# Cross-attention on one core: weights head by head ahead of the context, and larger pieces for Wv and x

## The chip, the cores and the metric

The kernel runs on one core of a Trainium2 chip. The metric is device time in microseconds (us), the median of several executions. Durations come from one profiled execution on the chip. PE is the matmul engine (PEld its weight loads, which overlap with its matmuls), DVE, ACT and POOL are the vector, scalar and general engines, SP is the engine that issues the DMA transfers; a name with q (SPq) is the engine's own sequencer.

## What is computed

One layer of cross-attention, all in float32, with B = 16, 256 queries of width 256 a batch, 77 keys of width 192 a batch, H = 8 heads of D = 256:

```python
Q = (img_embed @ Wq).reshape(B, -1, H, D).transpose(0, 2, 1, 3)
K = (sent_embed @ Wk).reshape(B, -1, H, D).transpose(0, 2, 1, 3)
V = (sent_embed @ Wv).reshape(B, -1, H, D).transpose(0, 2, 1, 3)
score = jnp.einsum('bhqd,bhkd->bhqk', Q, K) / math.sqrt(D)
score = jnp.where(mask, score, -jnp.inf)
attn = jax.nn.softmax(score, axis=-1)
ctx = jnp.einsum('bhqk,bhkd->bqhd', attn, V).reshape(B, -1, H * D)
out = ctx @ Wo + img_embed
return (out - mu) * jax.lax.rsqrt(var + EPS) * gamma + beta
```

img_embed is x (16 x 256 x 256), sent_embed the context (16 x 77 x 192), and the mask has one integer per key.

## The kernel before

The kernel multiplies weights together first. For each head, G = Wk Wq^T / 16 (192 x 256) takes the place of Wq and Wk, and U = Wv Wo (192 x 256) that of Wv and Wo. The 192 rows are held as 128 (A: gA, uA) and 64 (B: gB, uB). Then for a batch, a = G^T c^T (keys turned into the width of x), scores = x a, and the output is attention times vw = c U, plus x, normalised.

**Start (L441 to L621).** The transfers are issued in this order, all on SP but the first: the first two of eleven context blocks on ACT (L449), the other nine (L450), Wq and Wk for head 0, then head 1, then two heads at a time (L453 to L459), Wv in 24 transfers of pieces of 128 bytes (L460 to L468, already laid out for DVE's transposes of 32x32 blocks), Wo in four (L469), the mask (L472), and x of the first group of four batches, turned by blocks, in eight transfers of 128-byte pieces (L475, L155). PE's order is written by hand: 20 transposes of the identity that keep it busy (L484), the context's transposes pc (L492), then by head the transposes of Wq and Wk (p_wqT and p_wkT, L524) and the product pg (L538), one head of transposes ahead; then the B rows of G for all heads (ph, L548), a of the first group (pa, L186 and L200), U's A rows (pu, L538) and B rows (pw, L548), and the last 13 keys' vw of all batches (pr, L265 and L273), which go by way of a scratch in DRAM into vr (L287, L292). Between these, ACT and DVE in turn copy results out of PSUM (L138, L140); DVE turns Wv in place (wvT, L584) between the two halves of pa's copies and x (xT, L164) before pr's. POOL copies the second halves of cB and uB (L503, L599) and then computes the additive mask, bias (L602 to L617).

**Main loop (L632).** For each batch: scores of two tiles of 128 queries (ps, L306, 128x32 tiles of PE), shift and maximum (L320, L327, L328), exponential (L335), vw of the next batch (pv, L228 and L239), a quarter of the next group's a (pa), weights (L341 to L349), turned on DVE (L359), attention times vw (po, L371), and normalisation (L383 to L428). x of the next group is loaded once a group (load_xT) and turned on DVE.

All PSUM tiles come from one ring of eight banks, so a matmul that begins a tile waits until the tile of eight allocations earlier has been copied out. A float32 matmul is two records in the profile. A form like 64*32 after the names is the tile of PE's array that the instruction uses: rows by columns; instructions on different tiles run at once. Tiles that carry the same tag share storage: wo's load waits until the weights that lay there have been read, and the tiles for x's rows (xg) are first used for the turned Wq and Wk.

The U stage of before, L535 to L540 with L586 to L594, computes one head at a time over 128 rows:

```python
of_weights(pu[:, h % 2, :], wvT[:, h], slice(P), lambda dc: wo_part(h, dc))
```

Of the kernel before, what the change touches and what calls it, by code (L numbers as in the profile page):

```python
# [8 lines left out]
F32 = mybir.dt.float32  # L9
I32 = mybir.dt.int32  # L10
AF = mybir.ActivationFunctionType
ALU = mybir.AluOpType
# [33 lines left out]
def kernel(  # L46
# [25 lines left out]
    KR = S2 - KM  # L72
    BK = 32
    NM = P // BK
    PW = (NF + 1) * BK
    RB = 8
    assert KM == 2 * BK and NM == NF and 2 * KR <= BK
# [48 lines left out]
    def half(i):  # L126
        return slice(i * LB, (i + 1) * LB)
# [18 lines left out]
    def in_two(name, shape, g):  # L146
        return pools[g % 2].tile(shape, F32, tag=f"{name}{g % 2}", name=f"{name}_{g}", bufs=1)

    def load_blocks(dst, src):

        dst = dst.rearrange("p a (m q) -> p a m q", q=BK)
        src = src.rearrange("(m r) (a i q) -> a i r m q", r=BK, q=BK, i=P // BK)
        for a in range(dst.shape[1]):
            for i in range(P // BK):
                nc.sync.dma_start(dst[i * BK : (i + 1) * BK, a], src[a, i])  # L155

    def load_xT(g):
        xT_of[g] = in_two("xT", [P, 2, GT * P], g)
        load_blocks(xT_of[g], x.rearrange("b s d -> (b s) d")[g * GT * P : (g + 1) * GT * P, :])

    def transpose_x(g, j):

        cols = xT_of[g][:, :, j * P : (j + 2) * P]
        nc.vector.transpose(cols, cols)  # L164


# [2 lines left out]
    def prepare_a(g, pairs, B_first=False):  # L169
# [6 lines left out]
        banks = []  # L176

        def cols(dc, i):
            return slice(dc * P + i * BK, dc * P + (i + 1) * BK)

        def part_A():
            if not B_first:
# [115 lines left out]
    def scores(t):  # L298
        g = t // GT
        j, bl = t % GT, (t // QT) % GB  # L300
        ps = [ps_mm.tile([P, 512], F32, tag="mm", name=f"ps_{t}_{a}") for a in range(2)]
        for m in range(NM):
            q = j * P + m * BK
            for dc in range(2):
                for i in range(NM):
                    nc.tensor.matmul(  # L306
                        ps[m // 2][i * BK : (i + 1) * BK, m % 2 * 2 * S2 : (m % 2 + 1) * 2 * S2],
                        xT_of[g][:, dc, q : q + BK],
                        flat(a_of[g][:, dc, bl, 2 * i : 2 * i + 2, :]),
                        start=(dc == 0),  # L310
                        stop=(dc == 1),
                    )
        ps_of[t] = ps
# [126 lines left out]

    early = ctx.enter_context(tc.tile_pool(name="early", bufs=1))  # L441
    pools[0] = turned = early
    with tc.tile_pool(name="wload", bufs=4) as ring, tc.tile_pool(name="wonce", bufs=1) as wp:
        c_sb = wp.tile([CR, NCR, DL], F32, tag="c", name="c_sb")
        wq_r = wq.rearrange("(t p) f -> p t f", p=P)
        wk_r = wk.rearrange("(t p) f -> p t f", p=LP)
        wo_r = wo.rearrange("(t p) f -> p t f", p=P)
        first = 2
        nc.scalar.dma_start(c_sb[:, :first, :], c_rows[:, :first, :])  # L449
        nc.sync.dma_start(c_sb[:, first:, :], c_rows[:, first:, :])  # L450
        wq_of, wk_of, wo_of = {}, {}, {}
        wvT = wp.tile([P, H, 2, DL], F32, tag="wvT", name="wvT")
        for n in range(NF):  # L453
            wq_of[n] = ring.tile([P, 2, 2 * D], F32, tag="w128", name=f"wq_{n}")
            wk_of[n] = ring.tile([LP, 2, 2 * D], F32, tag="w96", name=f"wk_{n}")
            for lo, hi in ((0, D), (D, 2 * D)) if n == 0 else ((0, 2 * D),):
                cols = slice(2 * n * D + lo, 2 * n * D + hi)
                nc.sync.dma_start(wq_of[n][:, :, lo:hi], wq_r[:, :, cols])
                nc.sync.dma_start(wk_of[n][:, :, lo:hi], wk_r[:, :, cols])  # L459
        wv_blocks = wv.rearrange("(m r) (a i q) -> m i r a q", r=BK, q=BK, i=NM)  # L460
        for m in range(DL // BK):
            for i in range(NM):
                nc.sync.dma_start(
                    wvT.rearrange("p h a l -> p (h a) l")[
                        i * BK : (i + 1) * BK, :, m * BK : (m + 1) * BK
                    ],
                    wv_blocks[m, i],
                )  # L468
        for n in range(NF):  # L469
            wo_of[n] = ring.tile([P, 4, DI], F32, tag="w128", name=f"wo_{n}")  # L470
            nc.sync.dma_start(wo_of[n], wo_r[:, 4 * n : 4 * n + 4, :])
        nc.sync.dma_start(  # L472
            bias_f.bitcast(I32), mask.rearrange("b k -> (b k)").partition_broadcast(P)
        )
# [6 lines left out]
            for i in range(n):  # L481
                nc.tensor.transpose(idle, ident, ident)

        keep_busy(20)  # L484
        for r in range(0, NCR, 2):
            if r == first:
                keep_busy(2)
            n = min(2, NCR - r)
            pc = ps_mm.tile([P, 4, P], F32, tag="mm", name=f"pc_{r}")
            for lc in range(2):  # L490
# [15 lines left out]

        nc.gpsimd.memset(vr, 0.0)


        wqT_of = [  # L510
            const.tile([P, H // 2, 2, DI], F32, tag=f"xg{i}", name=f"wqT_{i}") for i in range(2)
        ]
        wkT_of = [
            const.tile([P, H // 2, 2, DL], F32, tag=f"xg{i + 2}", name=f"wkT_{i}") for i in range(2)
        ]
        wqT = [wqT_of[h * 2 // H][:, h % (H // 2)] for h in range(H)]
        wkT = [wkT_of[h * 2 // H][:, h % (H // 2)] for h in range(H)]

        def turn_weight(dst, w_of, rows, h, tag):
            pt = ps_mm.tile([P, 4, P], F32, tag="mm", name=f"p_{tag}_{h}")  # L520
            for dc in range(2):
                for r in range(2):
                    lo = h % 2 * D + dc * P
                    nc.tensor.transpose(  # L524
                        pt[:, 2 * dc + r, :rows],
                        w_of[h // 2][:, r, lo : lo + P],
                        ident[:rows, :rows],
                    )
            evacuate(dst.rearrange("p a (r n) -> p (a r) n", r=2), pt[:, :, :rows])

        def turn_qk(h):
            turn_weight(wqT[h], wq_of, P, h, "wqT")
            turn_weight(wkT[h], wk_of, LP, h, "wkT")

        def of_weights(out, tT, rows, moving):  # L535

            for dc in range(2):
                nc.tensor.matmul(  # L538
                    out, tT[:, dc, rows], moving(dc), start=(dc == 0), stop=(dc == 1)
                )  # L540

        def rest_of_weights(tT, moving, name):

            banks = [ps_mm.tile([P, DI], F32, tag="mm", name=f"{name}_{n}") for n in range(NF)]
            for n in range(NF):
                for dc in range(2):
                    for i in range(2):
                        nc.tensor.matmul(  # L548
                            banks[n][half(i)],
                            tT[2 * n + i][:, dc, P:],  # L550
                            moving(2 * n + i, dc),
                            start=(dc == 0),
                            stop=(dc == 1),
                        )
            return banks

        turn_qk(0)
        for h in range(H):
            if h + 1 < H:
                turn_qk(h + 1)  # L560
            if h % 2 == 0:
                pg = ps_mm.tile([P, 2, DI], F32, tag="mm", name=f"pg_{h}")
            of_weights(pg[:, h % 2, :], wkT[h], slice(P), lambda dc: wqT[h][:, dc, :])
            if h % 2:
                nc.scalar.mul(gA[:, h - 1 : h + 1, :], pg, D ** -0.5)
        for n, pg in enumerate(rest_of_weights(wkT, lambda h, dc: wqT[h][:, dc, :], "ph")):
            if n % 2:
                nc.scalar.mul(gB[:, n, :], pg, D ** -0.5)
            else:
                nc.vector.tensor_scalar(gB[:, n, :], pg, D ** -0.5, None, ALU.mult)  # L570
        for g in range(NG):
            load_x(g)
            if g == 0:
# [3 lines left out]
        for n in range(0, NF, 2):  # L577
            part_A, part_B, copies = prepare_a(0, (n, n + 1), B_first=(n > 0))
            for part in (part_A, part_B)[:: -1 if n else 1]:
                part()  # L580
            for dst, src in copies():
                evacuate(dst, src)
            for h in range(2 * n, 2 * n + 4, 2):
                nc.vector.transpose(wvT[:, h : h + 2], wvT[:, h : h + 2])  # L584

        def wo_part(h, dc):  # L586
            return wo_of[h // 2][:, h % 2 * 2 + dc, :]

        for h in range(H):
            if h % 2 == 0:  # L590
                pu = ps_mm.tile([P, 2, DI], F32, tag="mm", name=f"pu_{h}")
            of_weights(pu[:, h % 2, :], wvT[:, h], slice(P), lambda dc: wo_part(h, dc))
            if h % 2:
                evacuate(uA[:, h - 1 : h + 1, :], pu)  # L594
        for n, pu in enumerate(rest_of_weights([wvT[:, h] for h in range(H)], wo_part, "pw")):
            for i, engine in enumerate((nc.scalar.copy, nc.vector.tensor_copy)):
                h = 2 * n + i
                engine(uB[half(i), h, :], pu[half(i)])  # L598
                nc.gpsimd.tensor_copy(uB[half(1 - i), h, :], uB[half(i), h, :])  # L599


        nc.gpsimd.tensor_scalar(bias_f, bias_f.bitcast(I32), 0.0, None, ALU.is_equal)  # L602
# [123 lines left out]
```

## Time and profile before

| | |
|---|---|
| median of 3 runs | 290.67 us (290.58 to 290.76) |
| profiled execution | 290.27 us |
| its span, first to last instruction | 288.4 us |
| PE busy | 278.7 us (97%) |
| DVE, POOL, ACT busy | 206.3, 123.7, 118.2 us |
| mean granted PE clock | 0.992 |
| DMA, mean over the span | 90 GB/s, 64377 packets, 46905 of them under 512 bytes |
| start, up to the first scores (ps) | 0 to 61.35 us |
| main loop, last PE row | to 272.18 us |
| end on DVE and ACT | to 288.4 us |

The span lies 1.9 us below the profiled execution's time, and that time 0.4 us below the median of the runs. A row of the chain of waits is start, length and what; a row of the timeline is start, length, engine, line, operation, output<-input, tile and shapes, count, and in brackets the idle time before it and what ended it; a row of the windows is stretch and length, then the busy time of PE, PEld, DVE, ACT and POOL with counts, the granted clock, the DMA engines' busy share and GB/s.

### The profile page before, as it was taken

The numbers are of one execution on the slowest core, as the hardware profiler recorded it, in microseconds if no ns is written. First come the engines' busy times: TensorE is split into PE (matmuls) and PEld (weight loads), VectorE is DVE, ScalarE is ACT, GpSimd is POOL, SyncE is SP. The second block draws the span as 40 slices with busy tenths as digits, with TensorE's granted clock in tenths as the row PEclk, the third lists the DMA queues.
The fourth block names the chain that finished last, engine by engine and source line by source line (L and its number), as shares of the span: only waits on it lengthen the run. The fifth ranks groups of instructions, "written<-read, shape, count | busy, mean of one in ns | idle before, by whom it ended". The sixth has DMA issues, their size and how long they took to land.

```text
span 288.4 us, 11416 instructions
## 1 busy us (share of the span) xinstructions
PE 278.7 (97%) x5132; PEld 177.5 (62%) x5132; DVE 206.3 (72%) x412; ACT 118.2 (41%) x203; POOL 123.7 (43%) x156
## 2 busy tenths in 40 slices
PE   8899999999999999999999999999999999999990
PEld 8795567364656575757575757575757567576550
DVE  0531453435768798989797989897979898898884
ACT  2452232032353535353535353535353534735531
POOL 1800002986554334344334242534342527658562
PEclk9999999999999999999999999999999999999996
DMA  7986798895859401910101009200000000010112
GB/s 201 314 193 95 143 328 117 244 352 147 189 141 139 81 4 39 139 47 5 37 5 35 6 28 142 47 13 25 18 22 22 19 22 24 19 40 2 39 39 73
DMA packets 64377, 25.90 MB, mean 90 GB/s; under 512 B 46905, under 2 KB 62857, under 8 KB 64329
## 3 DMA queue, kind: packets, MB, share of 16 engines
q1 hardware_dynamic: 64088, 25.01, 36.8%
q8 instruction: 40, 0.66, 1.0%
q10 hardware_dynamic: 240, 0.17, 0.2%
q14 instruction: 9, 0.07, 0.1%
HBM read 19.27 MB, written 5.90 MB: 87 GB/s over the span
## 4 chain that ended last, share of the span: by engine, by line
PE 90%; DVE 3%; DMA 3%; SPq 1%; ACT 1%; issue 1%; POOL 0%; POOLq 0%
PE ps L306 23%; PE po L371 22%; PE pa L186 12%; PE pv L228 10%; PE pa L200 6%; PE pv L239 6%; DMA wk<-in_L_xattn_Wk_dram 3%; PE pu L538 2%; PE pr L265 2%; PE pg L538 2%; PE pr L273 1%; PE ph L548 1%; PE pw L548 1%; PE p_wqT L524 1%; PE p_wkT L524 1%; DVE bn L385 1%
## 5 line engine op out<-in xcount | busy, mean ns | idle before, releaser
L328 POOL TENSOR_TENSOR s<-s,top 128x616 f32<-128x616 f32 x32 | 39.0, 1218 | 85.0 <-DVE top L327 77.2
L306 PE MATMUL ps<-a,xT 128*32 128x154 f32 x2048 | 70.0, 294 | 0.0
L306 PEld LDWEIGHTS ps<-a,xT 128*32 128x32 f32 x2048 | 66.4, 110 | 4.0 <-ACT stage L138 0.8
L349 POOL TENSOR_TENSOR p<-e,rden 128x512 f32<-128x512 f32 x64 | 50.4, 808 | 28.6 <-ACT a L664 25.5
L371 PE MATMUL po<-vw,pT 128*32 128x256 f32 x1024 | 61.5, 380 | 0.0
L371 PEld LDWEIGHTS po<-vw,pT 128*32 128x32 f32 x1024 | 31.8, 110 | 28.2 <-issue 5.5
L341 DVE TENSOR_REDUCE den<-e 128x8 f32<-128x616 f32 x32 | 25.5, 795 | 24.2 <-ACT e L335 24.2
L335 ACT ACTIVATE e<-s 128x616 f32<-128x616 f32 x32 | 23.0, 719 | 32.1 <-POOL s L328 32.1
L186 PE MATMUL pa<-cA,gA 128*32 128x308 f32 x512 | 35.8, 423 | 0.0
L320 DVE TENSOR_TENSOR s<-ps,bias 128x308 f32<-128x308 f32 x64 | 27.6, 464 | 7.3 <-POOL bias L617 4.7
L662 ACT COPY vw<-pv 128x512 f32<-128x512 f32 x32 | 18.6, 581 | 32.2 <-PE pv L239 32.2
L228 PE MATMUL pv<-uA,cA 128*32 128x512 f32 x256 | 30.4, 592 | 0.0
L186 PEld LDWEIGHTS pa<-cA,gA 128*32 128x32 f32 x512 | 16.4, 110 | 21.0 <-issue 6.6
L428 DVE SCALAR_TENSOR_TENSOR xg<-xg,rstd,bet 128x256 f32<-128x256 f32 x26 | 28.0, 1078 | 0.9
L396 ACT ACTIVATE std<-mv,eps 128x2 f32<-128x2 f32 (+1 forms) x17 | 5.0, 296 | 57.2 <-DVE mv L388 57.2
L359 DVE STREAM_TRANSPOSE pT<-p 128x640 f32<-128x640 f32 x32 | 25.1, 812 | 2.4 <-POOL p L349 2.4
L327 DVE TENSOR_REDUCE top<-s 128x8 f32<-128x616 f32 x32 | 25.4, 795 | 1.1
L371 PE MATMUL po<-vr,pT 128*32 128x256 f32 x256 | 19.7, 379 | 0.0
L396 ACT ACT_TABLE_LOAD x15 | 19.2, 1283 | 0.3
L200 PE MATMUL pa<-cB,gB 64*32 64x308 f32 x512 | 19.3, 419 | 0.0
L335 ACT ACT_TABLE_LOAD x14 | 18.0, 1283 | 0.2
L599 POOL COPY uB<-uB 64x256 f32<-64x256 f32 x8 | 3.2, 397 | 34.7 <-ACT uB L598 34.3
(75 smaller groups left out, 288.2 us busy)
## 6 DMA issues: line engine op xcount, KB each, us to landing
xT<-in_x_dram SPq DMA_DIRECT2D x32, 128.0 KB
xg<-in_x_dram SPq DMA_DIRECT2D x4, 1024.0 KB
out_dram<-xg SPq DMA_DIRECT2D x15, 256.0 KB
wo<-in_L_xattn_Wo_dram SPq DMA_DIRECT2D x4, 512.0 KB
scratch<-stage SPq DMA_DIRECT2D x16, 104.0 KB
vr<-scratch SPq DMA_DIRECT2D x8, 208.0 KB
wq<-in_L_xattn_Wq_dram SPq DMA_DIRECT2D x3, 512.0 KB
wvT<-in_L_xattn_Wv_dram SPq DMA_DIRECT2D x24, 64.0 KB
```

Of the source, the lines that this page charges most:

```text
L186: nc.tensor.matmul(flat(o[i * BK : (i + 1) * BK]), gA[:, h, cols(dc, i)], flat(cA[:, batches, :]), start=not B_first, stop=B_first,)
L200: nc.tensor.matmul(flat(banks[j + k][i * BK : (i + 1) * BK]), gB[half(k), h // 2, cols(dc, i)], flat(cB[half(k), batches, :]), start=B_fir ...
L228: nc.tensor.matmul(pv[k][i * BK : (i + 1) * BK], cA[:, b, k * BK : (k + 1) * BK], flat(uA[:, heads[i], :]), start=True, stop=False,)
L306: nc.tensor.matmul(ps[m // 2][i * BK : (i + 1) * BK, m % 2 * 2 * S2 : (m % 2 + 1) * 2 * S2], xT_of[g][:, dc, q : q + BK], flat(a_of[g][:, ...
L320: nc.vector.tensor_tensor(s[:, a * H // 2 : (a + 1) * H // 2], ps[a][:, : H // 2 * S2].rearrange("p (h k) -> p h k", k=S2), bias[:, b, :]. ...
L327: nc.vector.tensor_reduce(top, s, AX.X, ALU.max)
L328: nc.gpsimd.tensor_tensor(s, s, top.unsqueeze(2).to_broadcast([P, H, S2]), ALU.subtract)
L335: nc.scalar.activation(e, s_of.pop(t), AF.Exp)
L341: nc.vector.tensor_reduce(den, e, AX.X, ALU.add)
L349: nc.gpsimd.tensor_tensor(part, e_mh[:, :, :, keys], rden_mh.unsqueeze(3).to_broadcast(list(part.shape)), ALU.mult,)
L371: nc.tensor.matmul(po[i * BK : (i + 1) * BK], pT[:, n, i], vw_of[b][:, n // 2, n % 2, :] if n < NF else vr[:, b, :], start=(n == 0), stop= ...
L428: nc.vector.scalar_tensor_tensor(y, y, rstd, bet, ALU.mult, ALU.add)
```

## The change

- SP issues Wq and Wk of each head as two transfers (pieces of 1 KB), heads 0 to 7, and only then the whole context in one transfer. They go into wq_all and wk_all, one tile each.
- Wv comes in 16 transfers with pieces of 512 bytes: each piece is 128 consecutive columns of a row of Wv. DVE turns it in place in blocks of 32x32 whose elements lie 16 bytes apart. Wo comes with four consecutive rows (4 KB) to a partition, into wo_all, which shares storage with wq_all.
- 14 identity transposes instead of 20, and none between the context blocks. PE begins with the weights; ph is done after heads 3 and 7 for two pairs each; the context's transposes follow G.
- U is computed for two heads at once: rows 0 to 63 of the array are one head and rows 64 to 127 the other, four steps n over the contraction, and the output in blocks of 32 columns (64*32 tiles). The two heads write to different banks. pw likewise, two pairs of heads at a time.
- x of a group comes in four transfers with pieces of 256 bytes instead of eight with pieces of 128. The order of its columns in blocks changes, and gA's columns (cols in prepare_a) with it.
- One Exp of one column is put at the start on ACT.

The core of the diff:

```diff
     def load_xT(g):
-        xT_of[g] = in_two("xT", [P, 2, GT * P], g)
-        load_blocks(xT_of[g], x.rearrange("b s d -> (b s) d")[g * GT * P : (g + 1) * GT * P, :])
+        xT_of[g] = in_two("xT", [P, GT * NM, 2, BK], g)
+        rows = x.rearrange("b s d -> (b s) d")[g * GT * P : (g + 1) * GT * P, :]
+        rows = rows.rearrange("(m r) (i n) -> i r m n", r=BK, i=NM)
+        for i in range(NM):
+            nc.sync.dma_start(
+                xT_of[g][i * BK : (i + 1) * BK].rearrange("p m n q -> p m (n q)"), rows[i]
+            )
...
-            return slice(dc * P + i * BK, dc * P + (i + 1) * BK)
+            return slice((2 * i + dc) * BK, (2 * i + dc + 1) * BK)
...
-                        xT_of[g][:, dc, q : q + BK],
+                        xT_of[g][:, j * NM + m, dc],
...
-        first = 2
-        nc.scalar.dma_start(c_sb[:, :first, :], c_rows[:, :first, :])
-        nc.sync.dma_start(c_sb[:, first:, :], c_rows[:, first:, :])
...
+        warm = wp.tile([P, 1], F32, tag="warm", name="warm")
+        nc.scalar.activation(warm, eps, AF.Exp)
+        wq_all = wp.tile([P, NF, 2, 2 * D], F32, tag="w128", name="wq_all")
+        wk_all = wp.tile([LP, NF, 2, 2 * D], F32, tag="w96", name="wk_all")
+        for h in range(H):
+            here, cols = slice(h % 2 * D, (h % 2 + 1) * D), slice(h * D, (h + 1) * D)
+            nc.sync.dma_start(wq_all[:, h // 2, :, here], wq_r[:, :, cols])
+            nc.sync.dma_start(wk_all[:, h // 2, :, here], wk_r[:, :, cols])
+        nc.sync.dma_start(c_sb, c_rows)
+
+        wvT = wp.tile([P, NF, NL, P], F32, tag="wvT", name="wvT")
+        wo_all = wp.tile([P, NF, 4, DI], F32, tag="w128", name="wo_all")
+        wv_blocks = wv.rearrange("(m r) (a i f) -> a i r m f", r=BK, a=NF, i=NM)
+        wo_rows = wo.rearrange("(a p n) f -> a p n f", p=P, n=4)
+        for a in range(NF):
             for i in range(NM):
+                nc.sync.dma_start(wvT[i * BK : (i + 1) * BK, a], wv_blocks[a, i])
+        for a in range(NF):
+            nc.sync.dma_start(wo_all[:, a], wo_rows[a])
...
-        keep_busy(20)
+        keep_busy(14)
...
+        turn_qk(0)
+        for h in range(H):
+            if h + 1 < H:
+                turn_qk(h + 1)
...
+            if h % 2:
+                nc.scalar.mul(gA[:, h - 1 : h + 1, :], pg, D ** -0.5)
+            if h % (H // 2) == H // 2 - 1:
+                rest_of_g(range((h - 2) // 2, (h + 1) // 2))
         for r in range(0, NCR, 2):
-            if r == first:
-                keep_busy(2)
...
-            for h in range(2 * n, 2 * n + 4, 2):
-                nc.vector.transpose(wvT[:, h : h + 2], wvT[:, h : h + 2])
+            for a in range(n, n + 2):
+                blocks = wvT[:, a].rearrange("p m (c n) -> p m n c", n=4)
+                nc.vector.transpose(blocks, blocks)
...
+        def wv_part(a, e, m, n):
+            return wvT[half(e), a, m].rearrange("p (c n) -> p n c", n=4)[:, n]
+
+        for a in range(NF):
+            if a % 2 == 0:
+                pu = [ps_mm.tile([P, 2, DI], F32, tag="mm", name=f"pu_{a}_{e}") for e in range(2)]
+            for n in range(4):
+                for m in range(NM):
+                    for e in range(2):
+                        nc.tensor.matmul(
+                            pu[e][m * BK : (m + 1) * BK, a % 2, :],
+                            wv_part(a, e, m, n),
+                            wo_all[half(e), a, n, :],
+                            start=(n == 0),
+                            stop=(n == 3),
+                        )
+            if a % 2:
+                for e in range(2):
+                    evacuate(uA.rearrange("p (a e) d -> p a e d", e=2)[:, a - 1 : a + 1, e], pu[e])
+        for pair in range(0, NF, 2):
+            pw = [ps_mm.tile([P, DI], F32, tag="mm", name=f"pw_{pair}_{e}") for e in range(2)]
+            for n in range(4):
+                for i in range(2):
+                    for m in range(NM, NL):
+                        rows = slice(i * LB + (m - NM) * BK, i * LB + (m - NM + 1) * BK)
+                        for e in range(2):
+                            nc.tensor.matmul(
+                                pw[e][rows],
+                                wv_part(pair + i, e, m, n),
+                                wo_all[half(e), pair + i, n, :],
+                                start=(n == 0),
+                                stop=(n == 3),
+                            )
```

## The prediction

> **What bounds the kernel now.** I read the busy shares first (PE 97%), then the chain of waits, because a share that high is only worth something if PE also carries the end of the work. It does: from 12.83 to 272.18 us the chain is PE instructions without a gap, and every microsecond taken out of PE's path before 61 us, where the main loop starts, comes off the end. From the chain, in order of time (start, length, what):
>
> ```profile
> 3.94 8.76 DMA wk<-in_L_xattn_Wk_dram
> 12.70 0.14 issue
> 12.83 0.52 PE p_wkT L524 x4
> 13.36 0.89 PE pg L538 x4
> 14.25 0.44 PE p_wqT L524 x4
> 14.68 0.33 PE p_wkT L524 x4
> ...
> 23.50 3.60 PE ph L548 x32
> 27.11 4.28 PE pa L186 x64
> 31.39 4.31 PE pa L200 x128
> 35.70 4.29 PE pa L186 x64
> 39.98 7.10 PE pu L538 x32
> 47.09 3.60 PE pw L548 x32
> ```
>
> Before 12.83 the end is set by a transfer: Wk of heads 2 and 3. From there one head costs 0.44 + 0.33 (transposes) + 0.89 (pg) = 1.66 us. Two things follow. A faster Wv or x load gives nothing by itself (PE never waits for either). What counts is when PE reaches pa (27.11) and what pu + pw cost (10.70).
>
> Next PE's weight loads at the start, in the timeline (start, length, ..., count):
>
> ```profile
> 1.34 4.13 PEld L482 LDWEIGHTS idle<-ident 128*128 128x128 f32 x20 [1.34 <-POOL ident masks.py:199]
> 5.46 0.82 PEld L492 LDWEIGHTS pc<-ident,c_sb 112*128 112x128 f32 x4
> 6.23 0.42 PEld L482 LDWEIGHTS idle<-ident 128*128 128x128 f32 x2
> 6.70 2.00 PEld L492 LDWEIGHTS pc<-ident,c_sb 112*128 112x128 f32 x18
> ```
>
> A 128x128 transpose takes 0.207 us here (4.13 / 20), and 0.11 later (0.44 / 4). The granted clock reads 1.00 throughout, so that column does not show it, but PE runs at half pace first. Of the last 18 (2.00 us), about two are slow: the change comes near 7.2 us, 5.85 us after PE began at 1.35.
>
> The windows give the bytes (last column GB/s):
>
> ```profile
> 0.00:3.00 3.00, 1.65 (x8) 1.66 (x9) 0.06 (x1) 1.28 (x1) 0.80 (x8) 1.00 0.27 54
> 3.00:5.00 2.00, 2.00 (x11) 2.00 (x10) 0.00 (x0) 0.00 (x0) 0.00 (x0) 1.00 1.08 335
> 5.00:9.00 4.00, 4.00 (x32) 3.95 (x31) 1.41 (x4) 1.63 (x5) 0.91 (x3) 1.00 1.12 286
> 9.00:12.00 3.00, 3.00 (x24) 2.36 (x22) 1.83 (x5) 1.43 (x4) 2.92 (x7) 1.00 1.06 315
> ```
>
> Summed: 162 kB at 3 us, 832 at 5, 1976 at 9, 2921 at 12. Wk of heads 2 and 3 ends 2781 kB into the queue (context 946, four half pieces 917, two pieces 917). That sum is passed at 11.56 us, and PE was released at 12.70: a transfer counts as landed 1.1 us after the byte count passes it.
>
> **The change, part by part.**
>
> *Weights first.* A head is 262 kB of Wq and 197 kB of Wk. On the same byte curve plus 1.1 us, Wq0 lands at 4.4, Wk0 5.0, Wq1 5.8, Wk1 6.4, heads 2, 3, 4 at 8.0, 9.6, 11.1, head 7 at 15.5, and the context (now last, 4616 kB) at 18.5. The pieces are 1 KB, as in the stretch 5 to 9 us at 286, so I keep that curve. PE: 14 idle transposes end at 1.34 + 14 x 0.207 = 4.2. Slow pace to 7.2: Wq0 4.4 to 5.2, Wk0 to 5.9, Wq1 to 6.7, Wk1 to 7.3, with no gap after 4.4. Then six heads of transposes (6 x 0.77 = 4.6), eight pg (7.1), ph (3.6), plus 0.3 because ph is now cut in two: a stage that changes the tile shape shows some 0.2 us over its streaming (pu 7.10 against 32 x 213 ns = 6.83). Sum 15.6, so G ends at 22.9. Each head has landed when PE gets there (turn 2 at 8.2, turn 3 at 9.9, turn 4 at 11.5), though by 0.2 to 0.4 us only. Then 22 context transposes at 0.115 (2.07 / 18) = 2.5: pa begins at 25.5 against 27.11, a **gain of 1.6 us**. The evictions keep pace as before (ACT 0.35, DVE 0.40 per group of 0.46 on PE). The context no longer leaves on ACT's queue (0.42 us of issue, beside nothing). The new Exp on one column stands where ACT is idle to 6.66 and already loads a table: nothing.
>
> *U in 64x32 tiles.* pu goes from 32 records to 256, pw from 32 to 128, with the same array work: 256 columns stream in 213 ns, eight tiles at once make 26.7 ns a record, 384 x 26.7 = 10.25, plus 0.2 for one shape change = 10.45 against 10.70. **Gain 0.25 us.** Nothing in the trace issues faster than pa's 64x32 rows, 4.31 / 128 = 33.7 ns, but these stream 308 columns, which is 257 / 8 = 32.1 by itself. Bounds: 26.7 (the array is full below that) and, as no record here reads weights at a stride, one weight load in full ahead of each matmul, (105 + 213) / 8 = 39.8, or with a load twice as long 52.9. I take the low end because of this row:
>
> ```profile
> 69.39 0.18 PEld L239 LDWEIGHTS pv<-uB,cB 64*32 64x32 f32 x16 [0.50 <-issue]
> ```
>
> Sixteen loads of 105 ns each fit in 0.18 us: loads of different tiles overlap almost wholly, so even a load of twice the length (210) hides behind its tile's own 213 ns.
>
> The weights are now every fourth float, 16 bytes apart. The Trainium skill, in "SBUF — State Buffer" (section "Door 1: The DMA port swizzle (why `[64,N]` ≈ `[32,N]`)"), says that each access in a new 16-byte line pays a penalty and that two accesses to a line are needed for full bandwidth; the same note calls a stride of four fp32 free. Its first half speaks against this change: by it the loads would double, and the U stage would go to the upper bounds if they did not overlap. No row here shows a strided weight load, so the overlap in the row above decides for me.
>
> *Wv's turning on DVE.* Same four instructions of 768 columns (956 ns), now at a stride. Nothing is gained, since the elements are as many. DVE is free for the first pair at 34.23 - 1.6 = 32.6 and pu begins at 38.4; the second pair starts at 38.9 and is due at 41.9 and 43.7. Twice the length (done 40.8, 42.7) is covered; at four times the last would end near 50 and hold pu back by some 6 us. The xT and pT rows (1.31 and 1.27 ns an element, gathered in blocks, against wvT's 1.24) are nearest, so I take nothing and leave the 6 us to the tail above the range.
>
> *Transfers.* Wv: 24 issues in 23.06 us become 16; landing was 34.7, will be well before 32. Wo now waits on SP until the last Wq transpose has read the shared buffer (19 us by the sum above); behind it on SP stand the mask and x. Its 2.1 MB took under 6 us at 362 GB/s, so it is there by 27, 11 us ahead of pu. x's eight issues (13.11 us) become four with as many pieces each; it was needed at 61.35 and landed at 52. Nothing on PE's path. Later groups' x hides in the loop, where DMA is 26% busy. The scores read the same 32-column blocks.
>
> *POOL.* pw's banks now fill in pairs, so the copies of uB end 2.05 us after pw instead of 1.6, and the mask arithmetic behind them on POOL with it. DVE's first shift waits for it (66.81); PE's third pa bank needs that shift's bank at 68.43 and it was free at 67.25. A delay of 0.45 leaves 0.7: nothing.
>
> *Sum.* 1.6 + 0.25 = 1.85 us. The profiled execution took 290.27 (span 288.4 and 1.9 around it), 0.4 under the median of the runs; 288.4 by it, **288.8 against the median**.
>
> **The rivals.**
>
> *Slower: the U records are not hidden.* At 33.7 ns a record pu + pw cost 12.9 (+2.2), with 1.6 gained: 291.3. With the load ahead of each matmul (39.8) 15.3: 293.7; at 52.9, 298.7. It decides from (10.70 + 1.6 - 0.2) / 384 = 31.5 ns. For it: no strided row, none under 32 ns. Against: sixteen loads in 0.18 us.
>
> *Slower: the context comes too late.* It now stands behind all the weights. PE wants it at 22.9, so everything must average 237 GB/s from 3 us on; below 216 the kernel is slower. At 200 it lands at 26.4: 292.3. Against: no single microsecond from 3 to 12 is under 266.
>
> *No change: PE stays slow.* If the gap after 4.2 starts the warm-up anew, full pace comes at 4.4 + 5.85 = 10.25, not 7.2; half of 3.05 is lost: 290.3. Against: a 1.0 us gap at 11.8 did not slow PE. That row is of a warm PE. In its own sentence: the Trainium skill ("TensorE: Matmul & The Clock Gate", Part 1) counts busy windows of about 3.4 us that run freely, by which a broken window could move full pace by 3.4 us, an estimated 1.7 us.
>
> *Better.* If full pace comes as early as 4.8, up to 1.2 us more, and 0.2 if landing lags less: 287.4.
>
> **How the numbers follow.** Forecast 288.8 (own range 288.1 to 289.5): 0.57. Better: 0.06. PE slow: 0.10. Context late: 0.07. U at about 33.7 ns: 0.11. U at 39.8 or worse, or wvT turned that slowly: 0.09. The range 287.4 to 291.6 leaves out the last and the late context, 0.16. About 0.2% (0.6 us) is what a measurement here can tell from no change: faster 0.63, same 0.10, slower 0.27.
>
> **What would show it.** pa's first row near 25.5; the first p_wqT near 4.4 and no DMA wait over 0.4 us after it; full pace by about 7.2; pu near 7.0 and pw near 3.5 us; DVE's wvT rows under 1.9 us each; the loop's rows unchanged. A PE wait on DMA ahead of pc, pu rows over 8 us, or 0.2 us transposes after 8 us would prove me wrong.

## The result: slower, with PE stopping for nothing the profile shows

The changed kernel takes 299.85 us (median of 4 executions, 297.46 to 301.44) against 290.62 (290.43 to 290.76) for the kernel before: ratio 1.031, 95% interval 1.024 to 1.038. The profiled execution took 299.74, its span is 297.6, so 9.47 us more than the profiled execution before. Executions of kernels whose PE stops in U differ from each other by several microseconds; those of the kernel before lie within 0.4 in this comparison, and between 290.08 and 294.33 in the widest of those below.

The chain of waits of the changed kernel, up to the first scores (start, length, what):

```profile
2.20 5.33 DMA wk_all<-in_L_xattn_Wk_dram
7.58 0.67 PE p_wkT L494 x4
8.25 1.76 PE pg L530 x4
10.01 0.85 PE p_wqT L494 x4
10.87 0.59 PE p_wkT L494 x4
11.46 0.89 PE pg L530 x4
...
27.77 4.29 PE pa L185 x64
...
40.65 5.05 PE pu L590 x174
45.69 3.17 issue
48.87 4.21 PE pu L590 x73
...
53.30 0.88 PE pw L607 x36
54.18 1.74 issue
55.91 2.81 PE pw L607 x84
58.73 7.04 PE pr L264 x16
...
69.38 4.33 PE ps L304 x128
...
94.18 4.04 PE ps L304 x121
98.22 0.70 issue
```

Read it by boundaries. pa begins at 27.77 instead of 27.11 (forecast 25.5), so 0.66 of the 9.47 is there before U begins. U (pu and pw) lasts from 40.65 to 58.73, 18.08 us instead of 10.70: +7.38. pr and pa are as long as before, and the first scores come at 69.38 against 61.35 (+8.03). PE's last row ends at 281.23 against 272.18 (+9.05): a 0.70 us stop inside ps makes most of what the loop adds.

The new thing is the word "issue" in the middle of a stage: PE's next instruction has all it needs by every semaphore and does not start. In the view of PE's waits (what waited, for what: us in total, times, longest) the two stops in U are the largest entries of all:

```profile
PE pu L590 <- issue: 3.2, 1, 3.2
PE pw L607 <- issue: 1.7, 1, 1.7
```

The stops take 4.91 us of U's 18.08. The rest is 13.17 us for 384 records. The first 174 records of pu run at 5.05 / 174 = 29.0 ns, near the forecast; the 82 after the first stop at about 4.4 / 82 = 54 ns. The windows say why (stretch and length, busy time and count of PE, PEld, DVE, ACT, POOL, granted clock, DMA share, GB/s):

```profile
7.00:9.00 2.00, 1.42 (x7) 1.24 (x8) 0.56 (x1) 0.33 (x1) 0.00 (x0) 0.72 1.08 285
9.00:12.00 3.00, 3.00 (x15) 2.64 (x14) 0.50 (x1) 0.59 (x1) 0.00 (x0) 0.62 1.12 274
49.00:51.00 2.00, 2.00 (x40) 0.97 (x47) 0.00 (x0) 0.00 (x0) 0.00 (x0) 0.50 1.06 358
```

The granted clock is 0.50 after the stop, and in windows of half a microsecond it stays there from 48.8 to 52.2; in the start it is 0.50 from about 7.9 to 11.3. So a stop is paid twice: once as a stop, once as about 2.2 us of records at half pace.

Where instructions come from is in the page's third part, which neither the prediction nor its rivals used: the queue of kind "instruction" (packets, MB, share of 16 engines). Before, then after:

```profile
q8 instruction: 40, 0.66, 1.0%
```

```profile
q8 instruction: 42, 0.69, 1.0%
```

The first part of the page gives PE 5132 matmuls and 5132 loads before, 5444 and 5444 after: 10264 / 40 = 257 and 10888 / 42 = 259 instructions a packet of 16.5 kB. PE's program arrives in pieces of about 256 instructions.

The trace also has the time of each such packet, and this ties them to the stops. In the changed kernel's view of the DMA, the windows from 46 to 47 us and from 53 to 54 us hold one packet each:

```profile
q8 instruction: 1, 0.02, 6.8%
```

```profile
q8 instruction: 1, 0.02, 7.1%
```

The first, of 16384 bytes, is moved from 46.26 to 47.34, and PE goes on at 48.87; the second from 53.28 to 54.41, and PE goes on at 55.91: both times 1.5 us after the packet. The same holds for all 16 stops of over 0.3 us in the eight profiled kernels that have any (the changed one and seven of the experiments): PE goes on 1.3 to 1.8 us after a packet of this queue has been moved. And if PE's semaphore instructions are counted with its loads and matmuls, each of the 16 lies a whole multiple of 256 instructions from the first one above. So these stops are waits for instructions.

### The profile page after: what moved, and what is told of

Same layout as the page of the kernel before. It is cut to its first block, busy times and chain, and to the rows that moved or that the text cites. A ratio compares the mean times of both kernels' runs of the same rounds, so it can differ in the third digit from the quotient of the medians.

```text
span 297.6 us, 12013 instructions
## 1 busy us (share of the span) xinstructions
PE 281.6 (95%) x5444; PEld 178.7 (60%) x5444; DVE 208.7 (70%) x412; ACT 118.2 (40%) x204; POOL 123.5 (42%) x156
## 4 chain that ended last, share of the span: by engine, by line
PE 90%; DVE 3%; issue 2%; DMA 2%; ACT 1%; POOL 0%; SPq 0%; POOLq 0%
PE ps L304 23%; PE po L369 21%; PE pa L185 11%; PE pv L227 9%; PE pa L199 6%; PE pv L238 6%; PE pu L590 3%; PE pg L530 3%; PE pr L264 2%; DMA wk_all<-in_L_xattn_Wk_dram 2%; PE ph L511 1%; PE pw L607 1%; PE pr L272 1%; PE p_wqT L494 1%; PE p_wkT L494 1%
## 5 line engine op out<-in xcount | busy, mean ns | idle before, releaser
L326 POOL TENSOR_TENSOR s<-s,top 128x616 f32<-128x616 f32 x32 | 39.0, 1217 | 86.1 <-DVE top L325 77.2
L185 PEld LDWEIGHTS pa<-cA,gA 128*32 128x32 f32 x512 | 17.3, 110 | 19.9 <-issue 5.9
L238 PE MATMUL pv<-uB,cB 64*32 64x512 f32 x256 | 17.4, 601 | 0.0
```

Of the source, the lines that this page charges most:

```text
L185: nc.tensor.matmul(flat(o[i * BK : (i + 1) * BK]), gA[:, h, cols(dc, i)], flat(cA[:, batches, :]), start=not B_first, stop=B_first,)
L238: nc.tensor.matmul(pv[k][i * BK : (i + 1) * BK], cB[half(k), b, k * BK : (k + 1) * BK], flat(uB[half(k), heads[i], :]), start=False, stop= ...
L326: nc.gpsimd.tensor_tensor(s, s, top.unsqueeze(2).to_broadcast([P, H, S2]), ALU.subtract)
```

## The experiments

Diffs are against the changed kernel, unless they say otherwise. The theory after the first look: PE runs out of instructions. Its rivals: the transfers of x's rows (xg), which the earlier end of the loads moved into U; the weights at a stride of four floats; and the order of the loads.

**x's rows out of U's way.**

```diff
-        for g in range(NG):
-            load_x(g)
+        load_x(0)
...
                 load_xT(g)
+                load_x(g)
```

> The changed kernel, but x of groups 1 to 3 for the residual (xg, 1 MB each) is loaded inside the loop, beside load_xT, and only group 0 at the start; all else as changed. Theory S (PE's instructions come by DMA, 16 KB a piece, and a piece is late when PE runs through 256 instructions in 3.4 us while the xg transfers fill the DMA engines): the two stops of 3.17 and 1.74 us in U's stage go or fall under 1 us together, no 0.50 clock after them, pu near 7.1 and pw near 3.7 us, pa still at 27.8; total about 292 against 299.85. Rival W (the strided weight loads of the 64x32 tiles themselves hold PE): pu to pr stays at 18 us, total about 300.

Measured: 295.9 us (293.56 to 298.56; before on that chip 291.03), ratio 1.011 (1.002 to 1.020). The stops are still there, after the same numbers of PE records as in the changed kernel: 0.44 in pu, 4.16 in pw, 1.21 in ps, in a profiled execution that took 298.56, the longest of its four. The 4.16 us stop begins at 48.70 and ends at 52.85; from 50 to 52 us this kernel's DMA moved 17 GB/s:

```profile
46.00:48.00 2.00, 2.00 (x88) 1.81 (x80) 0.17 (x1) 0.49 (x1) 0.00 (x0) 1.00 1.11 279
50.00:52.00 2.00, 0.00 (x0) 0.00 (x0) 0.00 (x0) 0.00 (x0) 0.00 (x0) 1.00 0.08 17
```

This does not clear the traffic. Other transfers still fill the DMA engines up to 48 us, and the packet that ends this stop is moved only at 50.30, when they have drained, 5.3 us after PE took up the piece before it. So x's later rows are not needed for a stop; that a full DMA makes stops longer fits both this and the median, 4 us below the changed kernel's, and is not shown by a run of its own.

**Fewer, wider tiles for U.** One tile of 64 rows by 128 columns does the work of four, so that pu has 64 records and pw 64. The stride stays.

```diff
-        def wv_part(a, e, m, n):
-            return wvT[half(e), a, m].rearrange("p (c n) -> p n c", n=4)[:, n]
+        def wv_part(a, e, n, cols):
+            return wvT[half(e), a].rearrange("p m (c n) -> p n (m c)", n=4)[:, n, cols]
...
-                for m in range(NM):
-                    for e in range(2):
+                for e in range(2):
...
-                            pu[e][m * BK : (m + 1) * BK, a % 2, :],
+                        pu[e][:, a % 2, :],
```

> The changed kernel with U in 64x128 tiles (pu, 64 records instead of 256) and 64x64 tiles (pw, 64 instead of 128), the same strided Wv and the same transfers. Theory S: 256 matmul and load instructions fewer per 7 us, so no stop or one under 1 us. By the changed kernel's loads (133 ns for 32 strided columns against 105 plain, so about 1.67 ns a column more for each further one) a 128-column load takes about 290 ns, over its matmul's 213, so pu is load-bound at about 9.5 us, pw 3.6; total about 294.5. Rival W (stride holds PE in small tiles): still a stop or a slow stage of 15 us or more, total 298 or more.

Measured: 291.76 (290.18 to 293.52) against 291.03, ratio 1.001 (0.997 to 1.005). Its chain has no stop:

```profile
39.43 7.77 PE pu L589 x64
47.20 3.68 PE pw L604 x64
```

Nearly the whole loss is gone with the 256 records. pu is 0.67 over before's 7.10, less than the 9.5 expected: a load of 128 columns at the stride takes 325 ns (190 for 128 plain ones in pg) and hides for the most part behind the other half's matmul.

**More idle transposes ahead of the weights.** `keep_busy(24)` for `keep_busy(14)`.

> The changed kernel with 24 idle transposes at the start instead of 14, nothing else. Theory H (the idle PE between 4.8 and 7.6 us lets a slow clock stand until 11.3): PE is busy to 6.3 us, full pace near 7.2, no 0.50 in the granted clock before 12 us, pa's first row at about 26.2 instead of 27.77; U's stops remain, total about 298.3. Rival (the head is bound by the transfers alone): pa at 27.8 or later, total about 300.

Measured: four executions from 291.06 to 299.92 (median 296.63), too far apart for a ratio. The profiled one is the fastest, 291.06: PE is at full pace from about 4.5 us on, pa begins at 26.06, pu has no stop and pw a short one:

```profile
38.94 7.10 PE pu L590 x256
46.03 1.25 PE pw L607 x34
47.28 0.58 issue
47.86 2.85 PE pw L607 x94
```

Undisturbed, pu's 256 records take 7.10 us, 27.7 ns each: the forecast's 26.7 with its 0.2 for the start. So the array does what the prediction said, when instructions are there. The three other executions take 5 to 9 us more; that they stop more is likely, but they left no profile.

**Context first, the rest as changed.** The context's two transfers and its transposes go ahead of the weights, with 20 + 2 idle transposes as before.

```diff
+        nc.scalar.dma_start(c_sb[:, :2, :], c_rows[:, :2, :])
+        nc.sync.dma_start(c_sb[:, 2:, :], c_rows[:, 2:, :])
         for h in range(H):
...
-        nc.sync.dma_start(c_sb, c_rows)
```

> The changed kernel with the order at the start undone: the context first (two blocks on ACT's queue, nine on SP's), its transposes before the weights', 20 idle transposes and 2 more after the first pair, as before the change; the weights still head by head, U and the piece sizes as changed. Theory: pa's first row near 27.1 as before the change (27.0), U's stops remain since U and the xg transfers are as changed; total about 299. Rival (weights first costs more than 0.7 us in the later stages): total under 297.

Measured: 299.2 (298.11 to 301.78), ratio 1.028 (1.019 to 1.037). pa begins at 26.57, no later than in kernels with the weights first and no slow clock (26.56 in the kernel with wide tiles). So no gain from the order of the loads can be seen; with one profile a kernel, a few tenths of a microsecond would not show. The stops stay:

```profile
41.02 3.72 PE pu L593 x126
44.74 2.36 issue
47.10 4.31 PE pu L593 x86
...
52.49 1.65 issue
54.15 2.85 PE pw L610 x90
```

The places tell more than the lengths. PE reaches U eight records later in its program here (22 idle transposes against 14), and the first stop comes after 38 + 126 = 164 pu records, ten earlier than the 174 of the changed kernel. Counted from PE's first record, the three stops lie at 592, 719 and 1483 here and at 594, 720 and 1485 there. Counted as instructions (a load and a matmul a record, and PE's semaphore instructions), the stops come after 1217, 1473 and 3009 in both kernels: the distances are one piece of 256 and six. The stops sit where one piece ends, wherever that falls in the work.

**Plain weights in the same small tiles.**

```diff
-            return wvT[half(e), a, m].rearrange("p (c n) -> p n c", n=4)[:, n]
+            return wvT[half(e), a, m, n * BK : (n + 1) * BK]
```

> The changed kernel with U's 64x32 tiles reading 32 adjacent columns of the turned Wv instead of every fourth (so U is not the reference's U); all counts, tiles and transfers as changed. Theory S, revised after the late x did not remove the stops: PE's instructions come 256 at a time (q8 packets of 16 KB), a piece is there 4.5 to 8 us after the one before it began, and U in 64x32 tiles uses one up in 3.4 us whatever its operands are. It expects stops of 2 to 6 us in all at the same records (174 of pu, 45 of pw), total 295 to 300. Rival W (strided loads) expects no stop, pu + pw 10.5 us, total 291 to 292.

Measured: 298.9 (296.0 to 300.37; before 290.56), ratio 1.027 (1.023 to 1.032). The loads fall to 106 ns. Of the three stops, the one at record 594 is down to 0.03 us; those at 720 and 1485 stay, 3.91 and 0.98 us long:

```profile
39.98 4.90 PE pu L590 x174
44.88 0.03 issue
44.91 2.56 PE pu L590 x81
...
47.69 0.91 PE pw L607 x37
48.60 3.91 issue
52.51 5.33 PE pw L607 x84
```

The stride is not the cause of the stops. 174 records in 4.90 against 5.05 with it: 0.9 ns a record is all that it costs.

**64x64 tiles, strided.** As the wide tiles, with pu in two column halves (128 records).

> The changed kernel with U in 64x64 tiles (pu 128 records, pw 64), strided as changed. Theory S: 256 instructions last 6.8 us in pu, so no stop or one under 1 us; a load of 64 strided columns takes 190 ns (as pw's in the wide tiles did), under the 213 of its matmul, so pu 7.0 to 7.2 and pw 3.6 to 3.7; total 290.5 to 291.5. Rival W: a stop or a slow stage of over 13 us, total above 294.

Measured: 290.99 (290.31 to 294.01), ratio 1.003 (1.000 to 1.005).

```profile
39.55 7.13 PE pu L590 x128
46.68 3.45 PE pw L605 x64
```

No stop in U; one of 0.35 us in ps, at 74.75.

**U's small tiles alone, on the kernel before.** Everything is the kernel before, but pu is cut into 64x32 tiles with plain weights.

```diff
-            of_weights(pu[:, h % 2, :], wvT[:, h], slice(P), lambda dc: wo_part(h, dc))
+            for dc in range(2):
+                for m in range(NM):
+                    for k in range(2):
+                        nc.tensor.matmul(
+                            pu[k][m * BK : (m + 1) * BK, h % 2, :],
...
```

(The core of the edit: 256 records of 64 rows, two banks.)

> The kernel before, with only its pu stage cut into 64x32 tiles (256 records instead of 32, plain columns; the lower half of each contraction goes to a bank that is left out, so U holds half its sum); transfers, order and pw as before. Theory S: the instructions of pu alone make PE run dry: a stop of 1 to 4 us in pu or in pw, then slow records; total 293 to 298. Rival W, or a theory that needs the changed transfers: no stop, total as the kernel before within 0.5 us.

Measured: 294.33 (293.63 to 296.71), ratio 1.014 (1.011 to 1.018).

```profile
40.41 4.88 PE pu L595 x166
45.29 1.69 issue
46.98 2.80 PE pu L595 x90
```

The stop, at record 594 once more, comes with the tiles alone: none of the changed loads, pieces or orders is in this kernel. A second one, 1.24 us, is in ps. Together with the two kernels before it this holds in both directions.

**A version to beat both.** Wv turned by DVE into a tile of its own, so that weights lie side by side, wide tiles and 24 idle transposes:

```diff
+        wvt = wp.tile([P, NF, 4, DL], F32, tag="w96", name="wvt")
...
-                blocks = wvT[:, a].rearrange("p m (c n) -> p m n c", n=4)
-                nc.vector.transpose(blocks, blocks)
+                nc.vector.transpose(
+                    wvt[:, a].rearrange("p n (m c) -> p m n c", c=BK),
+                    wvT[:, a].rearrange("p m (c n) -> p m n c", n=4),
+                )
...
-            return wvT[half(e), a].rearrange("p m (c n) -> p n (m c)", n=4)[:, n, cols]
+            return wvt[half(e), a, n, cols]
```

> The changed kernel with U in 64x128 and 64x64 tiles, Wv turned by DVE into a tile of its own so that the weights lie side by side, and 24 idle transposes. Expected if the two costs found so far are all: pa's first row at 26.1 (as with 24 idle transposes before), pu 7.1 (load 190 ns instead of 326, under 213), pw 3.6, no stop, first scores near 60.4 against 61.35 before the change; about 1.0 us under the kernel before. Rival (something later takes the gain back, by POOL's mask or the transfers): same as before within 0.2 us.

Measured: 292.11 (291.64 to 292.79), ratio 1.005 (1.003 to 1.007). pu fell to 7.11 us and the first scores came at 60.85, half a microsecond ahead of before. Then ps stopped:

```profile
85.65 3.90 PE ps L304 x114
89.55 1.60 issue
91.15 0.59 PE ps L304 x11
```

That is the forecast's miss in small: the half microsecond won by the first scores is lost to one late piece of program in the loop.

The same with pu in 64x64 tiles (128 records):

> The changed kernel with Wv turned into a tile of its own, 24 idle transposes, and U in 64x64 tiles: pu has 128 records, 64 more than in the wide tiles of the earlier run with Wv turned apart, at the same time on the array. By theory S this changes only where the 256th instructions fall: the stop of 1.60 us in that run's scores (before PE's matmul 1232) must go from there; with 10 records more than the strided 64x64 run, which stopped 0.35 us before matmul 974, one of at most 0.5 us may come in the scores near 75 us. Expected: pa at 26.1 to 26.6, pu 7.1, pw 3.5, first scores 60.4 to 60.8, total 290.0 to 290.6, at or 0.5 us under the kernel before. Rival (the stop belongs to the scores of that batch, for instance to x's transfer then): again 1.5 us near 90 us, total near 292.

Measured: 290.16 (289.72 to 291.64) against 290.8 on that chip, ratio 0.998 (0.995 to 1.000), with pu 7.07 us, pw 3.45 and no stop. pa came at 27.13 and the first scores at 61.19, both later than expected: PE waited 1.4 us for Wk in the start. It is the best version here, equal to the kernel before or 0.2% under it.

**x in 256-byte pieces alone, on the kernel before.**

> The kernel before with only x's pieces changed: four transfers of 256-byte pieces a group instead of eight of 128, and the order of columns that goes with them. PE's instructions are as many and in the same order. Expected: no stop of PE, first scores as before the change, total within 0.2% of the kernel before. Rival (a shorter x transfer moves the xg transfers forward and these hold up PE's instructions): a stop on PE of over 0.5 us and total over 291.2.

Measured: 292.15 (289.93 to 295.39), ratio 1.004 (1.001 to 1.007). The profiled execution took 290.95 and has no stop. Its first scores come at 62.12, 0.77 us later than before and not as expected, but all of the delay is there at pa (27.88 against 27.11), where Wk of heads 2 and 3 landed late, ahead of any load of x. The slower executions, up to 295, left no profile, and those of the kernel before reach 293.41 in this comparison. Whether x's pieces cost anything stays open.

## Why the prediction was wrong

**The step that failed: "U in 64x32 tiles", a gain of 0.25 us.** It priced 384 records by the array (26.7 ns), by the fastest row (33.7) and by their weight loads (39.8, 52.9). It did not price their supply. U went from 64 records to 384, so from 128 PE instructions to 768: half a piece of program became three, each run through in 128 x 26.7 = 3.4 us. The fastest 256 instructions before are ps's 128 records in 4.19 us and pa's 128 in 4.31, and that was a row to be weighed: nothing in the trace showed that instructions arrive in 3.4. From the chain of the kernel before:

```profile
86.14 4.19 PE ps L306 x128
```

Measured, the stage took 18.08 us instead of the forecast 10.45; 4.91 of it stops, some 2.2 the half clock after the first one, the rest small. In place of records limited by the array alone, the runs show PE waiting for its next 256 instructions, 3.17 and 1.74 us in U.

The array's part of the step was nearly right: 27.7 to 29.5 ns a record in the long stretches ahead of a stop, where instructions were there and the clock was full. So was the overlap of the loads, read off the row of sixteen loads in 0.18 us. Strided loads did get longer, 133 ns in the undisturbed stretches against 106 plain, and stayed hidden. As to the line rule weighed there (the Trainium skill, "SBUF — State Buffer", section "Door 1: The DMA port swizzle (why `[64,N]` ≈ `[32,N]`)"): its penalty is real, 325 ns against 190 for 128 columns, and its clause that a stride of four fp32 is free is not borne out; the doubling that the prediction read out of it was not reached; but it was not what decided.

**The rival that came nearest in number was wrong in kind.** "The U records are not hidden" had 298.7 for loads of double length in line. The kernel with plain weights keeps nearly the whole loss (1.027 of 1.031, intervals overlapping), so the loads had next to no part in it. A matching number is not a mechanism shown.

**Weights first: forecast -1.6, measured +0.66 at pa.** Two of its terms were off. The byte curve was that of the kernel before (335, 286, 315 GB/s), but the 1 KB pieces moved at 251 and 229 from 3 to 7 us; Wk of head 1 was there at 7.5, not 6.4, and its transposes ended at 8.25 instead of 7.3 (+0.95). And PE, left waiting 0.36 and 0.87 us in its warm-up, ran at half clock from 7.9 to 11.3; half of 8.25 to 11.3 is 1.5. 25.5 + 0.95 + 1.5 = 27.95 against 27.77. The second is the rival "PE stays slow", priced 1.5 and given 0.10. It is a matter of chance too: the kernels with x's rows late, wide tiles, 64x64 strided tiles and plain weights have the same start, and in their profiled executions the clock does not fall back there and pa came at 26.58, 26.56, 26.67 and 27.10. So without the half clock the gain was 0.0 to 0.55 us instead of 1.6, and the context-first kernel, at 26.57, shows none that is due to the order.

**Right.** DVE's turning of Wv at the stride grew from 956 to 1676 ns, below the 1.9 us up to which it was said to be covered, and no PE row waits for it. Wo, Wv and x's columns are waited for nowhere. "The context comes too late" did not happen: pc shows no wait. All three signs that were to prove the forecast wrong came: a wait of PE on DMA ahead of pc (0.87 us, for Wk of head 1), transposes of 0.2 us after 8 us (0.85 us for four at 10.01), and pu over 8 us.

**The rest of the loss.** With U in 64x64 tiles the changed kernel is at 1.003 (1.000 to 1.005): of 1.031, all but that goes with the small tiles.

**The time a piece takes.** In the changed kernel PE took up work at 48.87 and, one piece on, at 55.91: 7.0 us a piece; in the kernel with x's rows late 7.9, between 44.99 and 52.85. The packets' times split this. After each of the 16 stops, the packet for the next piece starts 1.05 to 1.13 us after PE goes on where the DMA engines' share in between is under 0.5 (five times), 2.1 to 4.5 us where it is above 1.0 (seven times), and 1.1 to 5.3 us between these. A packet mostly takes 0.9 to 1.5 us to move, 1.1 in the middle, and PE goes on some 1.5 us later. With an idle DMA that makes an estimated 1.1 + 1.1 + 1.5 = 3.7 us a piece, about what U's small tiles use one up in (256 x 27.7 / 2 ns = 3.5 us at their fastest), so that they leave nothing to spare; with a full one some 5 to 8.

**Open.** That the traffic delays the packets is read from these times; no run changes the traffic alone. Nor was it tried how far apart instructions must be to be always safe: ps, at 4.2 us for 256, stopped in seven of the eleven kernels profiled after the prediction, for 0.35 to 1.6 us, and not in the profiled kernel before.

## What to carry to other kernels

Before cutting one matmul into many smaller ones, count PE's instructions (a load and a matmul each) and the time in which 256 of them would run: an array that is equally full is no proof that the instructions come fast enough. Compare that time with the shortest the trace already sustains, and where the new one is below it, price a stop and the half clock after it. A stop called "issue" in the middle of a uniform stage, at a fixed count of instructions in several kernels, is a fetch and not a dependency; here the end of an instruction packet some 1.5 us before PE goes on confirms it.

## What the runs showed of the hardware

**Instructions come in pieces of 256, and not always in time.** Tile of U, time for 256 instructions, stops in U:

| tiles of U | ns a record | us for 256 | stops in U, profiled executions |
|---|---|---|---|
| 64x32 (pu, at full clock) | 28 to 32 | 3.5 to 4.1 | in all six kernels, the longest of each 0.58 to 4.16 us |
| 64x64 | 54 to 58 | 6.9 to 7.4 | none in two kernels (pu and pw), nor in pw of two more |
| 64x128 (pu) | 111 to 121 | 14 to 16 | none in two kernels |

The Trainium skill ("Runtime: NRT & Kernel Launch", section "🔬 Instruction fetch mechanics") says that instructions are refilled in blocks of 16 KiB, 256 of them, and the next block fetched while the current one runs, so that crossing a block is mostly hidden. The packets of 16384 bytes and the stops at multiples of 256 instructions agree with the block, and the packets' times with a lead of one block. "Mostly hidden" does not hold for dense small matmuls: stops of up to 4.16 us stand against it.

**The clock after a stop.** Stops of 1.69 and 1.74 us left PE at full pace afterwards (31 and 33 ns a record), stops of 2.36 and 3.17 at half (50 and 54 ns). The granted clock was 0.50 for 3.4 us after the 3.17 us stop and for 3.4 us in the start after waits of only 0.36 and 0.87. In the changed kernel the clock changes at 7.87, 11.28, 48.83 and 52.24, whole multiples of 3.41 us apart, so where a stop falls may count as well as its length; no run varies the place alone. The Trainium skill ("TensorE: Matmul & The Clock Gate", Part 1) has windows of about 3.4 us, and PE back at half clock after at least one idle one; the length of the slow stretch agrees, but here a stop of 2.36 us was enough.
